# Order of the opening work in a per-batch adapter kernel: table rows, row picks and the second group of x

## The chip, the cores and the metric

The kernel runs on one core of one Trainium2 chip. The metric is the time of one execution on the device in microseconds (us); several runs are made and their median is given. A core has five engines that run their own instruction streams: TensorE (PE, matrix products), VectorE (DVE), ScalarE (ACT), GpSimd (POOL) and SyncE (SP, which here only issues DMAs). They wait for each other by semaphores.

## What is computed

There are 128 batches of a 128 x 512 tile of x. Each batch has a language id from 0 to 8 that chooses one of ten adapters: a product with W1 (512 to 128), ReLU, a product with W2 (128 to 512), a residual, a layer norm with the language's gamma and beta, and once more x. All in float32.

```python
w1 = W1[language_ids]
w2 = W2[language_ids]
h = jnp.einsum('bsh,bha->bsa', hidden_states, w1) + b1[language_ids][:, None, :]
h = jax.nn.relu(h)
adapted = jnp.einsum('bsa,bah->bsh', h, w2) + b2[language_ids][:, None, :]
x = hidden_states + adapted
mean = jnp.mean(x, axis=-1, keepdims=True)
var = jnp.mean(jnp.square(x - mean), axis=-1, keepdims=True)
normed = (x - mean) * jax.lax.rsqrt(var + LN_EPS)
return normed * gamma[language_ids][:, None, :] + beta[language_ids][:, None, :]
```

The result is x plus what this function returns for x.

## The kernel before

**Tiling.** A batch is one tile with its 128 rows on the 128 partitions. x is loaded in groups of four batches (`load_x`, 1 MB, four buffers), the output is stored in pairs. W1 and W2 of all ten languages (2.6 MB each) are loaded once and stay in SBUF.

**Tables.** beta, gamma and b2 have ten rows each, and a batch needs one row of each on all 128 partitions. So the kernel spreads all 30 rows over the partitions at the start, into `beta_b`, `gamma_b` and `b2_b`. The 30 rows are split into three bfloat16 parts that add up to the float32 value (`parts`, lines 133 to 137), and `pick` (lines 130 and 131) is a matrix of zeros and ones, made from the identity, that adds the three parts of one row. `spread(r, copier)` (line 151) is one matmul of TensorE into a PSUM tile `row`, of which there are five buffers (pool `p_y`, shared with the batches' results `py`), and one copy of it to the table, by VectorE (L160) or ScalarE (L158). Rows 0 to 9 are beta, 10 to 19 gamma, 20 to 29 b2.

**Order.** Each engine's order is written out by hand: `keep` chains an instruction behind the one before it on its engine. In the opening, TensorE runs 12 matmuls on a tile of ones without use for the result (`spin`), then the transposes of batch 0 (`transpose_x`) and of b1, then 22 rows. Every third row goes to ScalarE, the others to VectorE; after row 5 stand the transposes of batch 1, and after each later row a short `spin`. Then ScalarE stages W1 of batches 0 and 1 (`stage_w1`, L186: a copy of the language's W1 to a fixed buffer, three buffers), and for batches 0 to 3 there follow the four W1 products (`down`, L214, one PSUM buffer `ph`), the transposes of batch b + 2 for b below 2 (one PSUM buffer `pxT`), ReLU (`relu`, L222), the copy of the transposed x (`copy_xT`, L195) and the rows that are left, three per batch. Then come the W2 products of batches 0 and 1 (`up`, L231, with b2 added by a row matmul, L230, in the first four batches and in every fourth after).

**Main loop.** From `i = 3` each turn holds, in TensorE's order, transposes of batch i, W1 products of batch i - 1, W2 product of batch i - 2, while VectorE and ScalarE do the residual, the statistics and the scaling of earlier batches, and GpSimd adds b2 to x (`add_b2`, L201) and beta to x (`add_beta`, L208). The first transposes in the loop are those of batch 4, right behind the W2 product of batch 2; they are the first use of x's second group. GpSimd's first `add_b2` is that of batch 4 too.

**DMA.** SP issues in this order: language ids, gamma, batches 0 and 1 of x, W1 in four parts, batches 2 and 3 of x, W2 in two parts, then x's groups 1 to 3. ScalarE issues beta, b2 and b1. A load of several rows is shared by all 16 DMA engines, and whoever waits for it waits for all 16 shares.

**VectorE at the start.** Only ScalarE's and SP's first instructions and TensorE's are chained by `keep` in the opening; the VectorE lines 119 to 137 stand unchained and are issued as: memsets, language ids (L119 to L122, wait for the ids' DMA), parts (L133 to L137), then `both` and `pick` (L130, L131).

Of the kernel before, what the change touches and what calls it, by code (L numbers as in the profile page):

```python
# [8 lines left out]
FP = mybir.dt.float32  # L9
BF = mybir.dt.bfloat16  # L10
I32 = mybir.dt.int32
AF = mybir.ActivationFunctionType
ALU = mybir.AluOpType
# [3 lines left out]
P = 128  # L17
G = 4
# [5 lines left out]
def cond_resid_kernel(ctx: ExitStack, tc: tile.TileContext, x, itok, W1, b1, W2, b2, gamma, beta, out):  # L24
# [8 lines left out]
    nc = tc.nc  # L33
    B, S, H = x.shape
    L, _, A = W1.shape
# [7 lines left out]
    def keep(ins):  # L43

        engine = ins.ins.engine
        if engine in last:
            tc.add_manual_dep(ins.ins, last[engine], behind, reason="kept order")
        last[engine] = ins.ins.name
        return ins

    const = ctx.enter_context(tc.tile_pool(name="const", bufs=1))
    xp = ctx.enter_context(tc.tile_pool(name="xp", bufs=4))
# [4 lines left out]
    st = ctx.enter_context(tc.tile_pool(name="st", bufs=6))  # L57
# [5 lines left out]
    xs = {}  # L63

    def load_x(g):
        t = xp.tile([P, G, H], FP, tag="x", name=f"x_{g}")
        keep(nc.sync.dma_start(out=t, in_=x[g * G : (g + 1) * G].rearrange("b s h -> s b h")))
        xs[g] = t

    def xb(b):  # L70
        return xs[b // G][:, b % G, :]


    ids = const.tile([1, B], I32, name="ids")
    rows = rp.tile([P, H], FP, tag="r", name="rows")
# [3 lines left out]
    x_0 = xp.tile([P, G, H], FP, tag="x", name="x_0")  # L79
    xs[0] = x_0  # L80

    def load_part(lo, hi):
        keep(nc.sync.dma_start(out=x_0[:, lo:hi, :], in_=x[lo:hi].rearrange("b s h -> s b h")))

    keep(nc.sync.dma_start(out=ids, in_=itok.rearrange("(o b) -> o b", o=1)))
    keep(nc.scalar.dma_start(out=rows[0:L, :], in_=beta))
    keep(nc.sync.dma_start(out=rows[L : 2 * L, :], in_=gamma))
    keep(nc.scalar.dma_start(out=rows[2 * L : 3 * L, :], in_=b2))
    load_part(0, 2)
    keep(nc.scalar.dma_start(out=b1r, in_=b1))  # L90

    warm = const.tile([P, 1], FP, name="warm")
    nc.vector.memset(warm, 1.0)
    keep(nc.scalar.activation(warm, warm, AF.Sqrt))
    for k in range(KC):
        keep(
            nc.sync.dma_start(out=w1[:, :, k, :], in_=W1[:, k * P : (k + 1) * P, :].rearrange("l p a -> p l a"))
        )
    load_part(2, G)
    for l in range(0, L, 5):  # L100
        keep(
            nc.sync.dma_start(
                out=w2[:, l * H : (l + 5) * H].rearrange("p (l h) -> p l h", l=5),
                in_=W2[l : l + 5].rearrange("l a h -> a l h"),
            )
        )
    for g in range(1, 4):
        load_x(g)

    ident = const.tile([P, P], FP, name="ident")  # L110
# [4 lines left out]
    nc.gpsimd.memset(ones, 1.0)  # L115


    wrap = const.tile([1, B], I32, name="wrap")
    nc.vector.tensor_scalar(wrap, ids, 0, L, ALU.is_lt, ALU.mult)  # L119
    lang = const.tile([1, B], I32, name="lang")  # L120
    nc.vector.tensor_tensor(lang, ids, wrap, ALU.add)
    nc.vector.tensor_scalar(lang, lang, 0, L - 1, ALU.max, ALU.min)  # L122


    R = 3 * L
    parts = const.tile([P, H], BF, name="parts")
    nc.vector.memset(parts.bitcast(mybir.dt.uint32), 0)
    pick = const.tile([96, R], BF, name="pick")
    both = st.tile([P, R], FP, tag="both", name="both", bufs=1)[:96, :]
    nc.vector.tensor_tensor(both, ident[:96, 0:R], ident[:96, 32 : 32 + R], ALU.add)  # L130
    nc.vector.tensor_tensor(pick, both, ident[:96, 64 : 64 + R], ALU.add)  # L131
    left = rp.tile([P, H], FP, tag="r", name="left")
    nc.vector.tensor_copy(parts[0:R, :], rows[0:R, :])  # L133
    nc.vector.tensor_tensor(left[32 : 32 + R, :], rows[0:R, :], parts[0:R, :], ALU.subtract)
    nc.vector.tensor_copy(parts[32 : 32 + R, :], left[32 : 32 + R, :])
    nc.vector.tensor_tensor(left[64 : 64 + R, :], left[32 : 32 + R, :], parts[32 : 32 + R, :], ALU.subtract)
    nc.vector.tensor_copy(parts[64 : 64 + R, :], left[64 : 64 + R, :])  # L137

    b1T = const.tile([P, L], FP, name="b1T")

# [10 lines left out]
    def spread(r, copier):  # L151
        t = (beta_b, gamma_b, b2_b)[r // L]
        row = p_y.tile([P, H], FP, tag="y", name=f"row_{r}")
        pick_r = pick[:, r : r + 1].to_broadcast([96, P])
        keep(nc.tensor.matmul(row, lhsT=pick_r, rhs=parts[:96, :], start=True, stop=True))
        dst = t[:, r % L * H : (r % L + 1) * H]
        if copier is nc.scalar:
            keep(nc.scalar.copy(dst, row))  # L158
        else:
            keep(nc.vector.tensor_copy(dst, row))  # L160
# [22 lines left out]
    def stage_w1(b):  # L183
        w1s[b] = wp.tile([P, KC, A], FP, tag="w1s", name=f"w1s_{b}")
        src = w1.rearrange("p l k a -> p (l k a)")[:, bass.ds(lid(b, ET.Activation) * (KC * A), KC * A)]
        keep(nc.scalar.copy(w1s[b].rearrange("p k a -> p (k a)"), src))  # L186

    def transpose_x(b):
        pxs[b] = p_x.tile([P, KC, P], FP, tag="xT", name=f"pxT_{b}")
        for k in range(KC):  # L190
            keep(nc.tensor.transpose(pxs[b][:, k, :], xb(b)[:, k * P : (k + 1) * P], ident))  # L191

    def copy_xT(b):
        xT[b] = tp.tile([P, KC, P], FP, tag="xT", name=f"xT_{b}")
        keep(nc.scalar.copy(xT[b], pxs.pop(b)))  # L195
# [14 lines left out]
    def down(b):  # L210
        phs[b] = p_h.tile([P, P], FP, tag="h", name=f"ph_{b}")
        for k in range(KC):
            keep(
                nc.tensor.matmul(  # L214
                    phs[b], lhsT=w1s[b][:, k, :], rhs=xT[b][:, k, :], start=(k == 0), stop=(k == KC - 1)
                )
            )
        del xT[b], w1s[b]

    def relu(b):  # L220
        hT[b] = tp.tile([P, P], FP, tag="hT", name=f"hT_{b}", bufs=6)
        keep(nc.scalar.activation(hT[b], phs.pop(b), AF.Relu, bias=b1T[:, bass.ds(lid(b, ET.Activation), 1)]))  # L222
# [191 lines left out]
    def spin(n, width):  # L414
        idle = p_s.tile([P, H], FP, tag="s", name="idle")
        for _ in range(n):
            keep(
                nc.tensor.matmul(
                    idle[:, :width], lhsT=ones, rhs=ones[:, 0:1].to_broadcast([P, width]), start=True, stop=True
                )  # L420
            )


    spin(12, H)
    transpose_x(0)
    transpose_b1()
    copy_xT(0)
    for r in range(22):
        spread(r, nc.scalar if r % 3 == 2 else nc.vector)
        if r == 5:  # L430
            transpose_x(1)
            copy_xT(1)
        elif r > 5:
            spin(1, H // 2)
    stage_w1(0)
    stage_w1(1)
    spin(3, H)
    for b in range(4):
        down(b)
        if b < 2:  # L440
            transpose_x(b + 2)
        relu(b)
        if b < 2:
            copy_xT(b + 2)
        for r in range(22 + 3 * b, min(25 + 3 * b, R)):
            spread(r, nc.scalar if r % 3 == 2 else nc.vector)
        stage_w1(b + 2)
    up(0)
    up(1)
# [1 line left out]
    for i in range(3, B + U):  # L451
        if i < B and i % G == 0 and i // G + 3 < NG:
            load_x(i // G + 3)
        b = i - U - 1
# [19 lines left out]
        g, half = divmod(b, 2)  # L474
# [80 lines left out]
```

## Time and profile before

| | |
|---|---|
| median of 3 runs | 320.62 us (320.58 to 321.12) |
| the profiled execution | 321.39 us, span 318.8 us |
| TensorE matmul busy | 305.1 us (96%) |
| VectorE busy | 300.7 us (94%) |
| ScalarE busy | 285.5 us (90%) |
| GpSimd busy | 280.6 us (88%) |
| first 25 us: VectorE, ScalarE, GpSimd busy | 17.15, 13.87, 3.36 us |

The span runs from the first to the last instruction; the time of a run has what lies around it as well. A line of a timeline reads: start, duration, engine, source line, operation, output <- inputs with their sizes, how many in a row (x4), and in brackets how long the engine had stood idle before it and what it waited for. In the part on waits, "issue" is a wait for nothing that the profile shows. PEld is TensorE's weight load, which runs beside its matmuls. Part 2 of the page cuts the span in 40 slices and shows each engine's busy tenths.

### The profile page before, as it was taken

To read this page: it belongs to the slowest core of one execution; us is meant where nothing else is said; L and a number is where in the kernel's file an instruction comes from. 1 tells how busy PE (TensorE), PEld (TensorE's weight loads), DVE (VectorE), ACT (ScalarE), POOL (GpSimd) and SP (SyncE) were. 2 spreads that over 40 slices of the span, in tenths; PEclk is the share of its full clock that TensorE was granted. 3 is DMA by queue.
4 is the path that set the end of the run, shared out by engine and by line. 5 is a ranking of instruction groups with operands and counts; after the bars stand their busy time and mean duration, and the time that the engine had idled before them with its cause. 6 is when DMAs were issued, how large, how long until landed. Compare 5 with 4: busy or idle time off the path is not lost. (4 is left out here: it accounts for less than half of the span.)

```text
span 318.8 us, 7184 instructions
## 1 busy us (share of the span) xinstructions
PE 305.1 (96%) x1889; PEld 226.0 (71%) x1889; DVE 300.7 (94%) x1000; ACT 285.5 (90%) x721; POOL 280.6 (88%) x234
## 2 busy tenths in 40 slices
PE   8998999999999999999999999999999999999960
PEld 3475777777777777777777777777777777777730
DVE  5946999999999999999999999999999999999995
ACT  2686989999999999999999999999999999999972
POOL 1306999999999999999999999999999999999873
PEclk9999999999999999999999999999999999999995
DMA  7997577577766666678666676678766666633324
GB/s 204 317 386 288 198 262 254 214 264 263 221 231 212 223 246 232 228 264 263 247 215 213 217 244 231 223 265 264 245 210 215 224 241 228 226 135 133 129 112 156
DMA packets 40986, 72.88 MB, mean 229 GB/s; under 512 B 1737, under 2 KB 6868, under 8 KB 40946
## 3 DMA queue, kind: packets, MB, share of 16 engines
q1 hardware_dynamic: 40886, 72.38, 66.4%
q8 instruction: 15, 0.25, 0.3%
q14 instruction: 25, 0.20, 0.2%
q10 hardware_dynamic: 60, 0.05, 0.1%
HBM read 38.86 MB, written 33.55 MB: 227 GB/s over the span
## 5 line engine op out<-in xcount | busy, mean ns | idle before, releaser
L208 POOL TENSOR_TENSOR o<-x,beta_b 128x512 f32<-128x512 f32 x128 | 162.0, 1278 | 10.6 <-DVE beta_b L160 10.6
L201 POOL TENSOR_TENSOR r<-x,b_b 128x512 f32<-128x512 f32 x93 | 118.8, 1277 | 20.0 <-DMA x<-in_x_dram 12.1
L214 PE MATMUL ph<-xT,w1s 128*128 128x128 f32 x1024 | 135.7, 275 | 0.3 <-ACT w1s L186 0.2
L231 PE MATMUL py<-w,hT 128*128 x256 | 130.9, 593 | 0.2 <-DVE o L290 0.2
L214 PEld LDWEIGHTS ph<-xT,w1s 128*128 128x128 f32 x1024 | 124.6, 192 | 2.6 <-ACT hT L222 1.3
L191 PEld LDWEIGHTS pxT<-ident,x 128*128 128x128 f32 x512 | 63.9, 141 | 67.1 <-issue 43.4
L281 DVE SCALAR_TENSOR_TENSOR py<-py,nmean,gamma_b 128x512 f32<-128x512 f32 x126 | 94.7, 752 | 0.3 <-issue 0.3
L290 DVE SCALAR_TENSOR_TENSOR o<-py,rstd,o 128x512 f32<-128x512 f32 x122 | 90.4, 741 | 1.4 <-DVE nmean L242 0.5
L249 ACT ACTIVATE sq<-py,nmean 128x512 f32<-128x512 f32 x124 | 85.3, 688 | 4.5 <-DVE nmean L242 2.9
L195 ACT COPY xT<-pxT 128x512 f32<-128x512 f32 x128 | 73.8, 577 | 12.1 <-PE pxT L191 10.1
L186 ACT COPY w1s<-w 128x512 f32 x128 | 79.5, 622 | 0.2 <-DVE gamma_b L160 0.2
L191 PE MATMUL pxT<-ident,x 128*128 128x128 f32 x512 | 77.0, 273 | 0.9 <-ACT xT L195 0.7
L237 DVE SCALAR_TENSOR_TENSOR py<-py,r 128x512 f32<-128x512 f32 x93 | 64.7, 695 | 2.5 <-POOL r L201 0.6
L222 ACT ACTIVATE hT<-ph,b1T 128x128 f32<-128x128 f32 x128 | 47.6, 372 | 1.1 <-PE ph L214 1.0
L231 PEld LDWEIGHTS py<-w,hT 128*128 128x128 f32 x256 | 41.6, 192 | 2.9 <-issue 0.9
L237 DVE SCALAR_TENSOR_TENSOR py<-py,x 128x512 f32<-128x512 f32 x35 | 24.2, 692 | 3.7 <-PE py L231 3.7
L249 ACT ACTIVATION_READ_ACCUMULATOR sq<-py,nmean 128x1 f32 x124 | 25.2, 203 | 0.0
L255 ACT ACTIVATE sd<-ssq,eps 128x2 f32<-128x2 f32 x62 | 18.3, 296 | 2.1
L242 DVE TENSOR_SCALAR nmean<-sum 128x1 f32<-128x1 f32 x128 | 18.7, 146 | 0.2
L230 PE MATMUL py<-parts,pick 96*128 96x512 bf16 x35 | 13.3, 381 | 0.0
L237 DVE DVE_READ_ACCUMULATOR py<-py,r 128x1 f32 x93 | 13.1, 141 | 0.0
L270 DVE TENSOR_TENSOR stat<-stat,y 128x2 f32<-128x2 f32 x62 | 12.8, 206 | 0.0
(54 smaller groups left out, 117.7 us busy)
## 6 DMA issues: line engine op xcount, KB each, us to landing
x<-in_x_dram SPq DMA_DIRECT2D x31, 1024.0 KB, 6.1
out_dram<-o SPq DMA_DIRECT2D x61, 512.0 KB, 3.5
w<-in_L_cond_W_dram SPq DMA_DIRECT2D x4, 640.0 KB, 6.6
w<-in_L_cond_W_dram SPq DMA_DIRECT2D x2, 1280.0 KB, 11.5
out_dram<-o SPq DMA_DIRECT2D x6, 256.0 KB, 2.2
x<-in_x_dram SPq DMA_DIRECT2D x2, 512.0 KB, 3.9
rows<-in_L_cond_beta_dram ACTq DMA_DIRECT2D x1, 20.0 KB
rows<-in_L_cond_gamma_dram SPq DMA_DIRECT2D x1, 20.0 KB
```

The costliest lines, as they stand in the source:

```text
L186: keep(nc.scalar.copy(w1s[b].rearrange("p k a -> p (k a)"), src))
L191: keep(nc.tensor.transpose(pxs[b][:, k, :], xb(b)[:, k * P : (k + 1) * P], ident))
L195: keep(nc.scalar.copy(xT[b], pxs.pop(b)))
L201: keep(nc.gpsimd.tensor_tensor(rs[b], xb(b), b2_b[:, bass.ds(v * H, H)], ALU.add))
L208: keep(nc.gpsimd.tensor_tensor(os[g][:, j, :], xb(b), beta_b[:, bass.ds(v * H, H)], ALU.add))
L214: nc.tensor.matmul(phs[b], lhsT=w1s[b][:, k, :], rhs=xT[b][:, k, :], start=(k == 0), stop=(k == KC - 1))
L222: keep(nc.scalar.activation(hT[b], phs.pop(b), AF.Relu, bias=b1T[:, bass.ds(lid(b, ET.Activation), 1)]))
L231: keep(nc.tensor.matmul(ys[b], lhsT=hT[b], rhs=w2[:, bass.ds(v * H, H)], start=not m, stop=True))
L237: keep(nc.vector.scalar_tensor_tensor(ys[b], ys[b], 1.0, r, ALU.mult, ALU.add, accum_out=s))
L249: keep(nc.scalar.activation(sq, ys[b], AF.Square, bias=nmeans[b], accum_out=ssqs[g][:, j : j + 1]))
L281: nc.vector.scalar_tensor_tensor(ys[b], ys[b], nmeans.pop(b), gamma_b[:, bass.ds(v * H, H)], ALU.add, ALU.mult)
L290: nc.vector.scalar_tensor_tensor(o, ys.pop(b), rstds[g][:, j : j + 1], o, ALU.mult, ALU.add)
```

## The change

Five things are changed.

- `both` and `pick` are made before the language ids and the parts, and VectorE's opening instructions are chained by `keep` in that order.
- One long `spin` fewer at the start, and rows 0 and 1 go ahead of the transposes of batch 0.
- Rows alternate: even ones are copied by VectorE, odd ones by ScalarE, with one short `spin` per pair. The transposes of batch 1 stand after row 7.
- 24 rows are made before W1 is staged (22 before), and two per batch in batches 0 to 2 (three, three and two before).
- x's second group (batches 4 to 7) is loaded by two DMAs of two batches each, into the same tile.

```diff
--- before.py
+++ after.py
@@ -80,7 +80,8 @@
     xs[0] = x_0
 
     def load_part(lo, hi):
-        keep(nc.sync.dma_start(out=x_0[:, lo:hi, :], in_=x[lo:hi].rearrange("b s h -> s b h")))
+        dst = xs[lo // G][:, lo % G : lo % G + hi - lo, :]
+        keep(nc.sync.dma_start(out=dst, in_=x[lo:hi].rearrange("b s h -> s b h")))
 
     keep(nc.sync.dma_start(out=ids, in_=itok.rearrange("(o b) -> o b", o=1)))
     keep(nc.scalar.dma_start(out=rows[0:L, :], in_=beta))
@@ -90,7 +91,7 @@
     keep(nc.scalar.dma_start(out=b1r, in_=b1))
 
     warm = const.tile([P, 1], FP, name="warm")
-    nc.vector.memset(warm, 1.0)
+    keep(nc.vector.memset(warm, 1.0))
     keep(nc.scalar.activation(warm, warm, AF.Sqrt))
     for k in range(KC):
         keep(
@@ -104,7 +105,11 @@
                 in_=W2[l : l + 5].rearrange("l a h -> a l h"),
             )
         )
-    for g in range(1, 4):
+    x_1 = xp.tile([P, G, H], FP, tag="x", name="x_1")
+    xs[1] = x_1
+    load_part(G, G + 2)
+    load_part(G + 2, 2 * G)
+    for g in range(2, 4):
         load_x(g)
 
     ident = const.tile([P, P], FP, name="ident")
@@ -115,26 +120,27 @@
     nc.gpsimd.memset(ones, 1.0)
 
 
-    wrap = const.tile([1, B], I32, name="wrap")
-    nc.vector.tensor_scalar(wrap, ids, 0, L, ALU.is_lt, ALU.mult)
-    lang = const.tile([1, B], I32, name="lang")
-    nc.vector.tensor_tensor(lang, ids, wrap, ALU.add)
-    nc.vector.tensor_scalar(lang, lang, 0, L - 1, ALU.max, ALU.min)
-
-
     R = 3 * L
     parts = const.tile([P, H], BF, name="parts")
-    nc.vector.memset(parts.bitcast(mybir.dt.uint32), 0)
+    keep(nc.vector.memset(parts.bitcast(mybir.dt.uint32), 0))
     pick = const.tile([96, R], BF, name="pick")
     both = st.tile([P, R], FP, tag="both", name="both", bufs=1)[:96, :]
-    nc.vector.tensor_tensor(both, ident[:96, 0:R], ident[:96, 32 : 32 + R], ALU.add)
-    nc.vector.tensor_tensor(pick, both, ident[:96, 64 : 64 + R], ALU.add)
+    keep(nc.vector.tensor_tensor(both, ident[:96, 0:R], ident[:96, 32 : 32 + R], ALU.add))
+    keep(nc.vector.tensor_tensor(pick, both, ident[:96, 64 : 64 + R], ALU.add))
+
+
+    wrap = const.tile([1, B], I32, name="wrap")
+    keep(nc.vector.tensor_scalar(wrap, ids, 0, L, ALU.is_lt, ALU.mult))
+    lang = const.tile([1, B], I32, name="lang")
+    keep(nc.vector.tensor_tensor(lang, ids, wrap, ALU.add))
+    keep(nc.vector.tensor_scalar(lang, lang, 0, L - 1, ALU.max, ALU.min))
+
     left = rp.tile([P, H], FP, tag="r", name="left")
-    nc.vector.tensor_copy(parts[0:R, :], rows[0:R, :])
-    nc.vector.tensor_tensor(left[32 : 32 + R, :], rows[0:R, :], parts[0:R, :], ALU.subtract)
-    nc.vector.tensor_copy(parts[32 : 32 + R, :], left[32 : 32 + R, :])
-    nc.vector.tensor_tensor(left[64 : 64 + R, :], left[32 : 32 + R, :], parts[32 : 32 + R, :], ALU.subtract)
-    nc.vector.tensor_copy(parts[64 : 64 + R, :], left[64 : 64 + R, :])
+    keep(nc.vector.tensor_copy(parts[0:R, :], rows[0:R, :]))
+    keep(nc.vector.tensor_tensor(left[32 : 32 + R, :], rows[0:R, :], parts[0:R, :], ALU.subtract))
+    keep(nc.vector.tensor_copy(parts[32 : 32 + R, :], left[32 : 32 + R, :]))
+    keep(nc.vector.tensor_tensor(left[64 : 64 + R, :], left[32 : 32 + R, :], parts[32 : 32 + R, :], ALU.subtract))
+    keep(nc.vector.tensor_copy(parts[64 : 64 + R, :], left[64 : 64 + R, :]))
 
     b1T = const.tile([P, L], FP, name="b1T")
 
@@ -421,17 +427,21 @@
             )
 
 
-    spin(12, H)
+    def spread_turn(lo, hi):
+        for r in range(lo, hi):
+            spread(r, nc.scalar if r % 2 == 1 else nc.vector)
+            if r % 2 == 1:
+                spin(1, H // 2)
+
+    spin(11, H)
+    spread_turn(0, 2)
     transpose_x(0)
     transpose_b1()
     copy_xT(0)
-    for r in range(22):
-        spread(r, nc.scalar if r % 3 == 2 else nc.vector)
-        if r == 5:
-            transpose_x(1)
-            copy_xT(1)
-        elif r > 5:
-            spin(1, H // 2)
+    spread_turn(2, 8)
+    transpose_x(1)
+    copy_xT(1)
+    spread_turn(8, 24)
     stage_w1(0)
     stage_w1(1)
     spin(3, H)
@@ -442,8 +452,8 @@
         relu(b)
         if b < 2:
             copy_xT(b + 2)
-        for r in range(22 + 3 * b, min(25 + 3 * b, R)):
-            spread(r, nc.scalar if r % 3 == 2 else nc.vector)
+        for r in range(24 + 2 * b, min(26 + 2 * b, R)):
+            spread(r, nc.scalar if r % 2 == 1 else nc.vector)
         stage_w1(b + 2)
     up(0)
     up(1)
```

`load_part`, `spread`, `transpose_x`, `copy_xT`, `stage_w1` and `spin` are otherwise as they were. In the order that comes out, TensorE has five idle matmuls fewer (26 for 31), and SP has one DMA more.

## Prediction

> **What bounds the kernel now.** I read the page's part 2 first: from the fourth slice of 40 to the second-last TensorE is at 9 tenths, and VectorE and ScalarE nearly so. So the middle has a limit of its own, and what this change touches (the first 27 us) can only shift it. Next the timeline of TensorE late in the run, to get the pace and see whether anything waits there.
>
> ```profile
> 289.21 0.60 PE L191 MATMUL pxT<-ident,x 128*128 128x128 f32 x4
> ...
> 291.40 0.60 PE L191 MATMUL pxT<-ident,x 128*128 128x128 f32 x4
> ...
> 293.59 0.60 PE L191 MATMUL pxT<-ident,x 128*128 128x128 f32 x4
> ...
> 296.00 0.60 PE L191 MATMUL pxT<-ident,x 128*128 128x128 f32 x4
> ```
>
> Batches start every 2.19 us, every fourth 0.22 later (the extra row matmul): 8.98 us per four batches, with no wait. That is TensorE's own work: transposes 0.44, four W1 products 0.89, the W2 product 0.86. The end is therefore TensorE's first uninterrupted moment plus fixed work. The timeline of TensorE over the start finds that moment:
>
> ```profile
> 16.39 1.16 PE L214 MATMUL ph<-xT,w1s 128*128 128x128 f32 x8 [0.23 <-ACT w1s L186]
> ...
> 22.97 0.38 PE L230 MATMUL py<-parts,pick 96*128 96x512 bf16 x1
> 23.19 1.02 PE L231 MATMUL py<-w,hT 128*128 x2
> ...
> 25.34 1.02 PE L231 MATMUL py<-w,hT 128*128 x2
> 26.59 0.63 PE L191 MATMUL pxT<-ident,x 128*128 128x128 f32 x4 [0.22 <-DMA x<-in_x_dram]
> 27.89 0.66 PE L191 MATMUL pxT<-ident,x 128*128 128x128 f32 x4 [0.68 <-ACT xT L195]
> ```
>
> The first W1 product waits for the staged W1 (16.39). The transposes of batch 4 wait for x's second group (26.59), those of batch 5 for the only transpose buffer (27.89), and from there nothing waits. Why W1 is staged so late is in the timelines of VectorE and ScalarE:
>
> ```profile
> 5.40 0.42 DVE L137 CAST parts<-left 30x512 bf16<-30x512 f32 x1
> 5.85 0.19 DVE L130 TENSOR_TENSOR both<-ident 96x30 f32<-96x30 f32 x1
> 6.07 0.19 DVE L131 TENSOR_TENSOR pick<-both,ident 96x30 bf16<-96x30 f32 x1
> ...
> 7.57 4.28 DVE L160 COPY beta_b<-row 128x512 f32<-128x512 f32 x7 [0.15 <-PE row L155]
> 11.76 4.26 DVE L160 COPY gamma_b<-row 128x512 f32<-128x512 f32 x7
> ```
> ```profile
> 13.52 0.59 ACT L158 COPY gamma_b<-row 128x512 f32<-128x512 f32 x1 [0.79 <-PE row L155]
> 14.90 0.59 ACT L158 COPY b_b<-row 128x512 f32<-128x512 f32 x1 [0.79 <-PE row L155]
> 15.72 1.14 ACT L186 COPY w1s<-w 128x512 f32 x2 [0.24 <-DVE gamma_b L160]
> ```
>
> VectorE copies without a gap, 0.61 us a row, while ScalarE idles before each of its rows: VectorE's two rows in three set the pace.
>
> Last the DMA landings, from the semaphore increments in the trace (16 parts each): W1 complete at 14.43, x's batches 2 and 3 at 15.78, W2 at 22.56. Of x's second group fifteen parts landed by 25.23 and the last at 26.45. The DMA view of 20 to 32 us names the cause, one packet of TensorE's program (16 KB, 22.54 to 23.63) on one of the engines:
>
> ```profile
> q8 instruction: 1, 0.02, 0.6%
> ```
>
> **What the Trainium skill says.** *Runtime: NRT & Kernel Launch*, "Instruction fetch mechanics": a program is refilled in blocks of 256 instructions by a DMA queue of its own, mostly hidden. The trace has 16 such packets, about 18 us apart; that at 22.54 isn't hidden, it delays x by 1.22 us. *DMA: Bandwidth & Descriptors*, "Queues, rings and completion order": each DMA engine takes the queues in turn, packet by packet, so one late engine holds back the whole count of 16; that fits the lone late part. *VectorE: DVE Perf Modes*, its table of costs, gives 120 + 512 cycles for such a copy from PSUM, 0.66 us; the trace has 0.68 alone and 0.61 in a row. *TensorE: Matmul & The Clock Gate*, on the clock gate: 427 ns for 512 columns while cold. The trace agrees: twelve idle matmuls, 5.30 us.
>
> **The change part by part.**
>
> *Row picks ahead.* `both` and `pick` (0.19 each, about 0.44 of the chain) move into VectorE's wait for `ids` (1.18 us, until 2.35). They need `ident`, ready at 1.44, so they end near 1.9: no cost. The parts still end at 5.82, since `rows` holds their start at 3.07. One idle matmul less (11 x 0.427) ends at 5.88, so row 0 starts near 5.95 instead of 7.14. Rows 0 and 1 now go before the transposes of batch 0, whose result nobody needs before W1 is staged.
>
> *Rows in turn.* 24 rows are 12 copies for each engine. VectorE takes row 0 at about 6.5, the small b1T copy (0.17), row 2 at 7.45, then one per 0.61: row 22 starts at 7.45 + 10 x 0.61 = 13.5. ScalarE's row 23 can be made once VectorE has freed row 18's buffer (5 buffers; row 18 ends near 13.0) and is copied 13.5 to 14.1. TensorE has 2 x 0.22 + 0.11 = 0.55 per pair: hidden, just. With 0.24 for the language id and its waits ScalarE is ready at 14.35; W1 landed at 14.43, plus 0.1 for the semaphore: staging starts at 14.5, 1.2 earlier. W1's landing is now the limit there; a faster copy would bring no more.
>
> *Batches 0 to 3.* One row fewer for TensorE in batches 0 and 1 (0.22 each), but ScalarE's relu, xT, row and W1 stage take 1.98 per batch (relu at 17.59, 19.57, 21.55) and are as many as before. TensorE's 0.89 + 0.44 + 0.44 = 1.77 lies below that: no gain. So the whole stretch moves by 1.2, and TensorE is ready for W2 at about 21.75 instead of 22.95.
>
> *What is late next.* W2, at 22.56, which the change leaves where it is. Before, a landing took 0.15 to reach TensorE (26.45 to 26.59), and the W2 product starts 0.1 after its weight load: I take 22.8 against 23.19. Of the 1.2 us, 0.8 is lost in that wait and 0.39 stays. The bound below is 22.65, above is the rival on W2.
>
> *x's second group in halves.* Three W2 products take 2 x 1.08 + 0.86 = 3.02, so TensorE reaches batch 4 at 25.85. At 387 GB/s (the DMA view) half a group, 524 KB, is 1.35 us: the first half lands at 25.1 if the fetch delays it as it did the group, at 23.9 if not. Either is in time. The second half, at 26.45, is needed by batch 6's transposes (30.36 before). SP's added issue stands in a backlog of over 10 us (W2 issued at 11.07, landed 22.56) and costs nothing; if the backlog were gone, 0.4.
>
> So batch 4's transposes move from 26.59 to 25.85: 0.74. ScalarE's xT copy follows at once (the square of batch 0 before it moves by 0.39 and ends at 25.7), and batch 5's transposes with it. Rows alone would have left 26.59 standing, and halves alone give about 0.35 (TensorE was busy to 26.2). GpSimd's first sum with b2 starts 1.35 earlier, which buys room but no time, as GpSimd's 7 x 1.23 = 8.63 per four batches lies below TensorE's 8.98.
>
> *Sum.* 318.8 - 0.74 = 318.1 for the span, 320.65 for the profiled run (321.39). The median is 0.77 below that run; taking the same difference: 320.62 - 0.74 = **319.9 us**.
>
> **The rivals.**
>
> *A, W2 arrives late (slower).* Five idle matmuls less are ten instructions fewer, yet TensorE runs 1.2 us earlier there, so the same fetch may be asked for before W2's last part is through. Price: the 1.22 us seen on x, W2 at 23.8, its product at 24.05, batch 4 at 27.1: 0.5 late, 321.1. It decides once W2 lands after 23.3. For it: the fetch started within 0.3 us of W2's landing. Against: with a backlog on the engine the later fetches start near the end of the transfer in progress (45.04 inside the x landing 44.52 to 45.43), which points to 22.5 again.
>
> *B, half the gain.* The fetch catches only W2's tail, as at 45 us, where the last part came 0.45 after the others: W2 at 23.0, 0.3 gained: 320.3.
>
> *C, more.* TensorE lost 0.31 and 0.29 near batches 14 and 22, after two of VectorE's register loads took 1.20 (41.4) and 1.13 us (59.7) instead of 0.6. With GpSimd earlier and x's loads released sooner these may not recur: 319.3. Against: I see no cause for them, so they may as well recur.
>
> *D, rows not faster.* TensorE's 0.55 of 0.61 per pair leaves little; should ScalarE's rows come late by 0.05 each, W1 is staged 0.6 later, which the wait for W2 still swallows. It has no weight of its own.
>
> **How the numbers follow.** Forecast 0.47 (own range 319.5 to 320.3), C 0.21, B 0.17, A 0.15. About 0.2%, 0.64 us, is what can be told from no change, so faster means under 319.98: three quarters of the forecast and C, 0.57. Slower means over 321.26: A with a further slow register load, 0.3, and what I overlook, 0.13. The rest, 0.30, is same. The range goes from C with a little more, 319.1, to A, 321.1.
>
> **What would show it.** Right: W1 staged at 14.5; W2's first product at 22.8 with a wait for W2 before it; batch 4's transposes at 25.8 without a wait for x; 2.19 us per batch after. Wrong: a W2 landing beyond 23 (A or B), a wait for x before batch 4, row copies that don't alternate at 0.61, or a TensorE that waits again after batch 5.

## The result and the profile after

| | before | after |
|---|---|---|
| median of 7 runs each | 320.79 us (320.33 to 321.74) | 319.72 us (319.49 to 320.55) |
| the profiled execution | 321.39 us, span 318.8 us | 319.72 us, span 318.0 us |

The ratio is 0.9967, with an interval of [0.9952, 0.9982]: the kernel became 0.33% faster, between 0.18% and 0.48%. In microseconds the medians differ by 1.07.

The timelines of VectorE and of ScalarE after the change (start, duration, engine, line, operation, and in brackets the idle time before it) show that the opening does what was asked of it:

```profile
1.48 0.19 DVE L128 TENSOR_TENSOR both<-ident 96x30 f32<-96x30 f32 x1 [0.30 <-POOL ident masks.py:199]
1.70 0.18 DVE L129 TENSOR_TENSOR pick<-both,ident 96x30 bf16<-96x30 f32 x1
...
13.26 1.27 DVE L166 COPY b_b<-row 128x512 f32<-128x512 f32 x2
```
```profile
10.42 2.76 ACT L164 COPY gamma_b<-row 128x512 f32<-128x512 f32 x5
13.14 1.13 ACT L164 COPY b_b<-row 128x512 f32<-128x512 f32 x2
14.50 1.14 ACT L192 COPY w1s<-w 128x512 f32 x2 [0.23 <-DMA w<-in_L_cond_W_dram]
```

The picks end at 1.88, ScalarE copies its last seven rows without a gap where it had idled 0.24 to 0.79 us before most of its rows, and W1 is staged at 14.50, held by nothing but W1's own landing (14.38). TensorE's timeline shows what became of these 1.2 us:

```profile
15.17 1.16 PE L220 MATMUL ph<-xT,w1s 128*128 128x128 f32 x8 [0.55 <-ACT w1s L192]
...
22.64 1.10 PE L237 MATMUL py<-w,hT 128*128 x2 [0.73 <-DMA w<-in_L_cond_W_dram]
...
24.88 1.02 PE L237 MATMUL py<-w,hT 128*128 x2
25.74 0.60 PE L197 MATMUL pxT<-ident,x 128*128 128x128 f32 x4
27.01 0.66 PE L197 MATMUL pxT<-ident,x 128*128 128x128 f32 x4 [0.68 <-ACT xT L201]
...
285.78 0.60 PE L197 MATMUL pxT<-ident,x 128*128 128x128 f32 x4
...
294.76 0.60 PE L197 MATMUL pxT<-ident,x 128*128 128x128 f32 x4
```

There is a new wait of 0.73 us for W2 (landed 22.51) before the first W2 product, and none for x before the transposes of batch 4 at 25.74: the first half of x's second group landed by 25.19, the second half by 26.55. The pace is unchanged, 294.76 - 285.78 = 8.98 us for four batches.

The span fell by 0.89 us. (The times of the two profiled executions differ by 1.67, because 2.5 us lie around the span in that of before and 1.8 in that of after.) TensorE's and SP's timelines split the 0.89 in three. The transposes of batch 5, from which on TensorE has no wait of this kind, start 0.88 earlier (27.89 to 27.01). On the way to the last batch TensorE slips, that is, a batch starts later than the pace, by 0.23 us once instead of by 0.31 and 0.29: 0.37 more. And the end took back 0.35: from the last transposes to the end of the span it was 318.85 - 302.57 = 16.28 before and 317.96 - 301.33 = 16.63 after.

### The profile page after: what moved, and what is told of

Read it like the earlier page. It is cut to its first block, busy times and chain, and to the rows that moved or that the text cites. A ratio compares the mean times of both kernels' runs of the same rounds, so it can differ in the third digit from the quotient of the medians.

```text
span 318.0 us, 7173 instructions
## 1 busy us (share of the span) xinstructions
PE 302.7 (95%) x1883; PEld 225.0 (71%) x1884; DVE 297.9 (94%) x995; ACT 289.1 (91%) x726; POOL 280.6 (88%) x234
```

## The experiments

The theory at first was the prediction's own: the new order of the rows brings TensorE to W2 early, W2's landing takes two thirds of that, and the halves of x are needed to keep the rest. Each run below was timed next to runs of the kernel before on the same chip; since the median of the latter differs a little between the three sets (320.73, 320.70, 320.51), the ratios are what to compare. They are worked out from all runs and lie up to about 0.1% from the quotient of the two medians. Where two kernels were not timed in one set, overlapping intervals decide nothing.

| kernel | median us | ratio to before | W2 product, batch 4's and 5's transposes start |
|---|---|---|---|
| before, profiled again | 320.51 | 1.0003 [0.9992, 1.0015] | 22.57, 26.08, 27.39 |
| rows only | 320.72 | 1.0009 [0.9994, 1.0025] | 22.63, 26.17, 27.48 |
| halves only | 319.63 | 0.9967 [0.9959, 0.9976] | 22.75, 25.84, 27.11 |
| changed, picks late | 319.69 | 0.9966 [0.9955, 0.9977] | 22.41, 25.50, 26.77 |
| changed, fetch early | 320.65 | 1.0008 [0.9994, 1.0022] | 23.49, 26.59, 27.86 |
| before, no short idle matmuls | 319.70 | 0.9965 [0.9951, 0.998] | 22.56, 25.65, 26.92 |
| changed, five languages | 319.05 | 0.9949 [0.9936, 0.9962] | 21.89, 24.91, 26.18 |
| old rows, halves, five languages | 319.50 | 0.9961 [0.9947, 0.9975] | 22.40, 25.42, 26.69 |
| changed, W2 product later | 319.32 | 0.9960 [0.9947, 0.9972] | 22.45, 24.94, 26.49 |
| the same, no short idle matmuls | 318.96 | 0.9946 [0.9931, 0.9962] | 22.43, 24.44, 25.95 |
| the same, six more on VectorE | 318.39 | 0.9937 [0.9914, 0.9961] | 22.67, 24.68, 26.20 |
| old rows, halves, product later, no short idle | 318.21 | 0.9931 [0.9911, 0.9951] | 22.42, 24.43, 25.95 |

### The two halves of the change apart

Rows only: the changed kernel with x's second group loaded whole.

```diff
-    x_1 = xp.tile([P, G, H], FP, tag="x", name="x_1")
-    xs[1] = x_1
-    load_part(G, G + 2)
-    load_part(G + 2, 2 * G)
-    for g in range(2, 4):
+    for g in range(1, 4):
         load_x(g)
```

> The changed kernel with x's second group loaded whole again. Theory (the moment that counts is batch 4's transposes, and they need x): W1 is staged at 14.5 and W2's first product starts at 22.6 as in the changed kernel, but batch 4's transposes stay near 26.5, and the time is that of the kernel before within 0.3 us. Rival (the rows alone carry the gain): transposes near 25.8 and 0.8 us or more faster than before.

Halves only: the kernel before with that edit the other way round.

> The kernel before with x's second group in two halves and nothing else. Theory: TensorE itself is busy to 26.2, so batch 4's transposes start at 26.2 instead of 26.6 and the time falls by about 0.35 us; the two parts of the change together (0.85) bring more than the sum of each alone (0 and 0.35). Rival (halves are all that matters): 0.8 us faster.

Rows only gave nothing (1.0009). TensorE's timeline of that kernel:

```profile
22.63 1.10 PE L233 MATMUL py<-w,hT 128*128 x2 [0.73 <-DMA w<-in_L_cond_W_dram]
...
26.17 0.63 PE L193 MATMUL pxT<-ident,x 128*128 128x128 f32 x4 [0.29 <-DMA x<-in_x_dram]
```

It waits twice, for W2 and for x. (Batch 4 starts before the 26.5 expected, because x's second group was complete at 26.04 here.) Halves only gave all of the gain (0.9967, as the whole change). Here are TensorE's timelines, first of the kernel with halves only, then of the kernel before profiled again:

```profile
1.18 4.97 PE L423 MATMUL idle<-ones 128*128 128x512 bf16 x12 [1.18 <-POOL ones L120]
...
15.92 1.16 PE L219 MATMUL ph<-xT,w1s 128*128 128x128 f32 x8 [0.22 <-ACT w1s L191]
...
22.75 1.10 PE L236 MATMUL py<-w,hT 128*128 x2
...
25.84 0.60 PE L196 MATMUL pxT<-ident,x 128*128 128x128 f32 x4
```
```profile
1.18 4.57 PE L418 MATMUL idle<-ones 128*128 128x512 bf16 x12 [1.18 <-POOL ones L115]
...
15.61 1.16 PE L214 MATMUL ph<-xT,w1s 128*128 128x128 f32 x8 [0.22 <-ACT w1s L186]
...
22.57 1.10 PE L231 MATMUL py<-w,hT 128*128 x2
...
26.08 0.63 PE L191 MATMUL pxT<-ident,x 128*128 128x128 f32 x4 [0.26 <-DMA x<-in_x_dram]
```

> The kernel before, unchanged, for another profile of it. Theory (how late the old rows run depends on when TensorE's clock rises: the twelve idle matmuls took 5.30 us in the profile of before, but 4.97, 4.46 and 4.15 in three kernels that open alike): the first W1 product lies between 15.6 and 16.4 and the first W2 product 6.8 later, but not before W2 has landed, at 22.5 to 23.2; batch 4's transposes start at 26.3 to 26.6 in any case, because they wait for x; the time is 320.7. Rival (the opening of the kernel before is always as late as in its profile, and was earlier in the others through the halves or the idle matmuls left out): 16.4 and 23.2.

The first line carries part of the explanation. The same twelve idle matmuls took 5.30 us in the first profile of before, but 4.97 and 4.57 here, and 4.46, 4.34 and 4.15 in other kernels that open the same way: they come 0.43 us apart while TensorE's clock is low and 0.22 once it is up, and the moment at which it rises differs between executions. The old rows follow that moment: the first W1 product at 16.39, 15.92, 15.61, and the first W2 product at 23.19, 22.75, 22.57, that is, 6.8 to 7.0 later. The picks set a floor to this: where the idle matmuls took only 4.15 us (the old rows with five languages, below), TensorE waited 0.44 us for the picks, and the first W1 product started at 15.61 all the same. In the last two of the three profiles, TensorE comes to W2 just as it has landed (22.61 and 22.43), with no faster rows. The second profile of before also missed one expectation: batch 4 started at 26.08 and not at 26.3 to 26.6, because x's second group was complete at 25.95 instead of 26.45.

The new rows are done when W1 lands, and so TensorE reaches W2 too early to profit in full: 22.64 with a wait of 0.73, where the old rows give 22.57 with hardly one in the second profile of before and 23.19 in the first. At this point the new rows bring anything from nothing to 0.55 us, depending on the opening that they are compared with.

Which opening is the usual one isn't shown. The span of the first profile, 318.8, is that of most runs of before (medians of 318.9, 318.75 and 318.7 in the three sets); that of the second is 318.3, and none of its 14 runs has a shorter one. A rival to "W2's landing takes it all" is therefore that the new rows do gain at the start and lose as much at the end: from the last transposes to the end every profile with the new rows takes 0.34 to 0.59 us longer, except in one kernel that was changed for this (see the end of this part). The equal times of rows only and before, and of halves only and the whole change, speak for some of this, as a loss at the end without a gain at the start would show in them as about 0.1%; but that is less than their intervals can tell.

The picks, the smallest part of the change, can be undone without a loss that shows:

```diff
-    keep(nc.vector.tensor_tensor(both, ident[:96, 0:R], ident[:96, 32 : 32 + R], ALU.add))
-    keep(nc.vector.tensor_tensor(pick, both, ident[:96, 64 : 64 + R], ALU.add))
...
     keep(nc.vector.tensor_copy(parts[64 : 64 + R, :], left[64 : 64 + R, :]))
+    keep(nc.vector.tensor_tensor(both, ident[:96, 0:R], ident[:96, 32 : 32 + R], ALU.add))
+    keep(nc.vector.tensor_tensor(pick, both, ident[:96, 64 : 64 + R], ALU.add))
```

> The changed kernel with the two operations that make the row picks put back behind the rows' parts, all else as in the changed kernel. Theory: the first row and all behind it up to the staging of W1 come 0.4 to 0.45 us later (W1's first product at about 15.6 instead of 15.17), the wait for W2 in front of its first product (0.73) takes this in, and the time stays at 319.7. Rival (the picks' move is part of the gain): 320.1.

The first W1 product went from 15.17 to 15.61, as expected, and the first W2 product starts at 22.41 with hardly a wait, right behind the landing (22.27). The ratio, 0.9966, is about that of the changed kernel (0.9967).

### Is the wait for W2 what takes the rows' gain?

The two kernels of this pair leave languages 5 to 9 out: ids are clamped to 0 to 4 and half of W2 is loaded, so that W2 is there by 19.2. One has the new rows, the other the old, both have the halves.

```diff
-    for l in range(0, L, 5):
+    for l in range(0, L // 2, 5):
...
-    w2 = const.tile([P, L * H], FP, name="w2")
+    w2 = const.tile([P, L // 2 * H], FP, name="w2")
...
-    keep(nc.vector.tensor_scalar(lang, lang, 0, L - 1, ALU.max, ALU.min))
+    keep(nc.vector.tensor_scalar(lang, lang, 0, L // 2 - 1, ALU.max, ALU.min))
```

> The changed kernel with language ids limited to 0 to 4 and only the first half of W2 loaded; the other languages' batches are computed with language 4. Theory (W2's landing is what comes late next): W2 is there at 19.1, its first product starts when TensorE is ready, 21.75, batch 4's transposes at about 24.8, and the time falls by a further 0.85 us against the changed kernel. Rival (something else holds batch 4, such as the row copies or ScalarE): transposes stay near 25.7 and the time as in the changed kernel within 0.2 us.

> The kernel before with x's second group in halves and with half of W2 loaded (languages 5 to 9 are left out, ids are clamped to 0 to 4): the old order of rows, in the setting where W2 is no longer awaited. Theory (the new order of rows brings the first W1 product 0.75 to 1.2 us forward, and in the changed kernel W2's landing takes it all): the first W2 product starts at 22.75 to 23.0 and batch 4's transposes at 25.85 to 26.1, against 21.89 and 24.91 with the new rows in the same setting; the time is 319.6 to 319.9 against 319.05 there. Rival (the new order of rows is worth nothing in any setting): 319.05.

TensorE's timeline of the kernel with new rows, then of the one with old rows:

```profile
21.89 1.02 PE L237 MATMUL py<-w,hT 128*128 x2
...
24.91 0.60 PE L197 MATMUL pxT<-ident,x 128*128 128x128 f32 x4
```
```profile
22.40 1.02 PE L236 MATMUL py<-w,hT 128*128 x2
...
25.42 0.60 PE L196 MATMUL pxT<-ident,x 128*128 128x128 f32 x4
```

With W2 out of the way the new rows bring both starts forward by 0.51 us. So they are worth something at the start where nothing holds TensorE at W2; in the full kernel W2's landing takes this away where the old rows open as early as they do here. The size was below the 0.75 to 1.2 us expected: the old rows opened early here too (the idle matmuls took 4.15 us). Of the 0.51, the spans show only 0.1 (316.9 against 317.0, and TensorE slips in neither): the new rows lose the other 0.42 at the end, see below. The ratios, 0.9949 and 0.9961, overlap in their intervals.

### Why halves help: TensorE's program fetch

The prediction named one packet of TensorE's program, 16 KB, as the cause of x's late sixteenth share. Two runs move it. In the first, the kernel before loses the 16 short idle matmuls between its rows, 32 TensorE instructions with their weight loads, and keeps x's second group whole:

```diff
-        elif r > 5:
-            spin(1, H // 2)
```

> The kernel before, without the 16 single idle matmuls between its rows (32 TensorE instructions fewer), nothing else. Theory (TensorE's program fetch at 22.54 us is what made x's second group 1.2 us late, and halves help only because they get the first half past it): with fewer instructions the same fetch comes some microseconds later, the whole second group is complete at about 25.2 instead of 26.45, batch 4's transposes start without a wait for x at 25.85 to 26.3 (26.59 before), and the time falls by 0.3 to 0.8 us, to 320.0 to 320.4. Rival (a second group loaded whole is late for its size): x complete at about 26.1 or later and the time stays at 320.7.

TensorE's timeline of that kernel, and its page's DMA part for 20 to 25.5 us:

```profile
22.56 1.10 PE L231 MATMUL py<-w,hT 128*128 x2 [0.24 <-DMA w<-in_L_cond_W_dram]
...
25.65 0.60 PE L191 MATMUL pxT<-ident,x 128*128 128x128 f32 x4
```
```profile
DMA packets 1072, 2.13 MB, mean 387 GB/s; under 512 B 32, under 2 KB 32, under 8 KB 1072
...
q1 hardware_dynamic: 1072, 2.13, 104.9%
```

No program packet is left in this stretch (it comes at 28.9 instead), the whole group is complete at 25.13 instead of 26.45, and batch 4 doesn't wait. The last of the 16 shares comes 0.11 us after the fifteenth, where it came 1.22 and 0.86 after it in the two profiles of before. The second of those is the one to compare with, as its first W2 product starts at 22.57 too: there batch 4 starts at 26.08, here 0.43 earlier. The ratio of this kernel, 0.9965, is about that of the changed kernel, with neither the new rows nor the halves, and better than the 0.3 to 0.8 us expected, partly since TensorE came to W2 early here (22.56, right behind its landing). The Trainium skill, *Runtime: NRT & Kernel Launch*, "Instruction fetch mechanics", has the fetch of 256-instruction blocks mostly hidden behind execution. TensorE indeed never stops for it in the profile of before; what isn't hidden is its 1.1 us on one of 16 DMA engines, in front of a load that all 16 must finish.

In the second run the changed kernel gets 33 narrow idle matmuls more, of the same total width, so that the fetch comes earlier:

```diff
-    spin(11, H)
+    spin(44, P)
```

> The changed kernel with its 11 opening idle matmuls of 512 columns made 44 of 128 columns: the same TensorE time, 66 instructions more ahead of everything. Theory (a fetch of TensorE's program holds up whatever transfer stands behind it on its DMA engine): the 16 KB packet comes before W2's second part instead of after it, near 18.8 instead of 22.5; W2's last part lands near 23.7 instead of 22.5, batch 4's transposes start near 26.9 instead of 25.7, and the time is 1.1 us above the changed kernel's, at or above the kernel before. Rival (a fetch is hidden wherever it falls): W2 and the time as in the changed kernel within 0.2 us.

```profile
23.49 1.10 PE L237 MATMUL py<-w,hT 128*128 x2 [1.12 <-DMA w<-in_L_cond_W_dram]
...
26.59 0.60 PE L197 MATMUL pxT<-ident,x 128*128 128x128 f32 x4
```

TensorE's timeline shows the price. The fetch now stands at 17.1, in front of W2, whose last share lands at 23.36 (22.51 in the changed kernel); the W2 product and batch 4 are 0.85 late (1.1 was expected), and the whole gain is gone (1.0008, and the median too is about that of before). Five of its 22 runs took 322.4 to 323.2 us; the one profile, of a run of 320.36, doesn't show why. This was the prediction's rival A: its mechanism is real, its price 0.85 us, and it didn't happen in the changed kernel, where the fetch stayed at 22.5.

### A version that beats both

If the end is the moment from which TensorE runs without a wait plus fixed work, the 0.68 us for which batch 5's transposes wait behind batch 4's is next. Batch 2's W2 product can fill it:

```diff
-        if i == 4:
-            up(2)
         if i > 3 and on(i):
             transpose_x(i)
+        if i == 4:
+            up(2)
```

> The changed kernel with batch 2's W2 product issued after batch 4's transposes instead of before them. Theory (the end is TensorE's first uninterrupted moment plus fixed work, so the 0.68 us for which batch 5's transposes wait for batch 4's xT copy is still lost): batch 4's transposes start once the first half of x has landed, at about 25.3, the W2 product fills the wait, batch 5's transposes start at about 26.6 instead of 27.01, and the time falls by 0.4 us against the changed kernel, to about 319.3. Rival (W2's products set VectorE's work, and VectorE is as late as TensorE): no gain, 319.7.

> As the run before this one, and without the single idle matmuls between the rows (22 TensorE instructions fewer or more), so that the program fetch comes later. Theory: the first half of x is no longer delayed by the fetch and lands at about 24; batch 4's transposes start at 24.9, batch 5's at 26.25 instead of 27.01, and the time falls by 0.75 us against the changed kernel, to about 319.0. Rival (VectorE is as late as TensorE, or the fetch lands on another load that is waited for): 319.4 to 319.7.

The second run also leaves out the short idle matmuls between the rows. TensorE's timeline of each:

```profile
24.94 0.63 PE L197 MATMUL pxT<-ident,x 128*128 128x128 f32 x4 [0.31 <-DMA x<-in_x_dram]
...
25.63 1.02 PE L237 MATMUL py<-w,hT 128*128 x2
26.49 0.60 PE L197 MATMUL pxT<-ident,x 128*128 128x128 f32 x4
```
```profile
22.43 1.10 PE L237 MATMUL py<-w,hT 128*128 x2 [0.68 <-DMA w<-in_L_cond_W_dram]
...
24.44 0.60 PE L197 MATMUL pxT<-ident,x 128*128 128x128 f32 x4
...
25.09 1.02 PE L237 MATMUL py<-w,hT 128*128 x2
25.95 0.61 PE L197 MATMUL pxT<-ident,x 128*128 128x128 f32 x4
```

With the edit alone the W2 product fills the wait, and batch 4 waits for x again, whose first half the fetch delays (24.81). With the fetch moved to 27.7 that wait is gone too, and batch 5 starts at 25.95, 1.06 before the changed kernel. The times are those expected (319.32 and 318.96), though the intervals overlap with that of the changed kernel.

> The kernel before (old order of rows) with x's second group in halves, batch 2's W2 product after batch 4's transposes, and without the single idle matmuls between its rows. Theory (W2's landing takes all of what the new order of rows brings, and the new order costs 0.3 us in the last stores): W2's product at 22.45 to 22.7, batch 5's transposes at about 26.0 as with the new rows (25.95), a final wait 2.9 us after VectorE's last start, and a time of 318.65 to 318.9, no worse than the 318.96 of the same with the new rows. Rival (the new rows are worth something here): 319.3 to 319.5.

The same with the old rows, which is the kernel before with the halves, the moved product and without short idle matmuls, gave 318.21 us, 0.9931, less than the 318.65 to 318.9 expected. TensorE's timeline starts alike:

```profile
22.42 1.10 PE L236 MATMUL py<-w,hT 128*128 x2
...
24.43 0.60 PE L196 MATMUL pxT<-ident,x 128*128 128x128 f32 x4
...
25.09 1.02 PE L236 MATMUL py<-w,hT 128*128 x2
25.95 0.62 PE L196 MATMUL pxT<-ident,x 128*128 128x128 f32 x4
```

It has the lowest median of all and none of the new order. In the two profiles its span is 0.75 shorter than with the new rows: 0.27 by fewer slips of TensorE on the way, 0.48 from the last transposes to the end (16.15 against 16.63). In the same set of runs the changed kernel with late picks, which starts as the changed kernel does, had 319.69 and an interval that begins above where this one ends (0.9955 against 0.9951). Against the same kernel with new rows the intervals overlap.

### What the new rows cost at the end

From the start of VectorE's last operation to the moment at which SP has seen the last store land, every kernel with the new rows took 3.22 to 3.29 us, every one with the old rows 2.85 to 2.98. A suspect is an 8 KB program packet. With new rows it starts 0.6 us after VectorE's last operation has started, in the last stores, with old rows 1.3 us before; and by the traces' count it comes after some 1346 of VectorE's instructions, of which there are 1350 with the new rows and 1356 with the old. Six one-column memsets at VectorE's start make up for the difference:

```diff
-    keep(nc.vector.memset(warm, 1.0))
+    for _ in range(7):
+        keep(nc.vector.memset(warm, 1.0))
```

> The fastest kernel so far (the changed kernel, batch 2's W2 product after batch 4's transposes, no single idle matmuls; 318.96 us) with six more one-column memsets on VectorE at its very start, where it waits for the identity anyway; nothing else. In all kernels with the new order of rows the final wait comes 3.22 to 3.28 us after VectorE's last operation starts, in those with the old order 2.87 to 2.95. Theory (an 8 KB packet of VectorE's program, asked for near its 1346th instruction, falls into the last stores since the new order gives VectorE six instructions fewer): the packet moves back by some 1 us against the end, the final wait comes 2.9 us after, the time falls by 0.3 us to about 318.65. Rival (the last stores are slower for another reason, such as which engine's turn or the layout of the rows): 3.25 us and 318.96, or a little more by the six memsets.

The DMA view of the 2.25 us that follow the start of VectorE's last operation, without and with the six:

```profile
q1 hardware_dynamic: 335, 0.62, 73.0%
q14 instruction: 1, 0.01, 0.9%
```
```profile
q1 hardware_dynamic: 351, 0.65, 76.5%
```

The packet (q14) left the window as expected, which shows that it is VectorE's. The final wait fell from 3.23 to 3.05 us, half of what was expected, and the stretch from the last transposes to the end from 16.63 to 16.35 (16.15 to 16.28 in the six kernels with old rows, 16.62 to 16.74 in the seven with new ones). The ratio fell from 0.9946 to 0.9937, but the intervals overlap, and TensorE's slips, 0.39 us without the six and 0.06 with them, could make all of that difference. So one profile gives 0.2 to 0.3 us for the packet, the times can't confirm it, and what makes up the rest of the loss stays open.

## Why the prediction was right, and where it failed

**The time.** 319.9 was forecast and 319.72 measured, faster, inside the forecast's own range. The sum was made of one term, 0.74 us for batch 4's transposes. In the two profiles that term measured 0.85 (26.59 to 25.74), and two more that the sum didn't have nearly cancel, which is luck: 0.37 gained by slips, 0.35 lost at the end. The 0.77 us by which the profiled run of before lies above the median, and which the prediction took off, lie around the span and not in it: 2.5 us there, against 1.8 in most runs of before. (Two products and sums are off by a little: 22.8 + 3.02 is 25.82, and 7 x 1.23 is 8.61. Neither matters.)

**Row picks, rows in turn.** Held line by line: picks ended at 1.88 (1.9), staging began at 14.50 (14.5), W1's landing became its limit, batches 0 to 3 kept ScalarE's pace (1.97, then 1.76 between relus, for 1.98).

**What is late next.** Held: W2 landed at 22.51 and its product began at 22.64 after a wait, 0.16 earlier than the 22.8 taken.

**Halves.** Batch 4 at 25.74, for 25.85, without a wait for x. The fetch stood where it was expected and delayed the first half (to 25.19, for 25.1), which was in time.

**The step that failed** is the split: "Rows alone would have left 26.59 standing, and halves alone give about 0.35 (TensorE was busy to 26.2)". Rows alone gave nothing, as said, but halves alone gave 1.10 us (320.73 to 319.63), three times the 0.35 and as much as the whole change. Two terms were wrong. The 26.2, like the 0.39 us put down to the rows at W2, was read from one opening of before; with the same rows TensorE was through with its third W2 product at 25.66 in the second profile and at 25.84 with halves only. And the loss of the new rows at the end was put at nothing. How much of the 1.10 us is due to which isn't shown: the span with halves only is 0.58 shorter than in one profile of before and 1.13 shorter than in the other, of which batch 5's earlier start makes 0.28 and 0.78. The right reading of the change is: halves 0.33%, rows nothing on balance, with a loss at the end and a gain at the start of 0 to 0.55 us.

**The rivals.** A (W2 late through the fetch): real, but it needs the fetch well before W2's end. The run that put it at 17.1 lost 0.93 us; in the second profile of before it began at 21.79, and W2's last share landed at 22.43, only 0.09 after the one before it. B (half the gain by W2's tail): W2 landed at 22.51, no. C (fewer slips): half of it, 0.37 of the 0.60 in the pair of profiles. It isn't the change's doing as far as the runs show: slips of 0.06 to 0.6 us occur with old and new rows, and four profiles had none. D (rows late by 0.05 each): no.

## What to carry to other kernels

An opening that depends on the moment at which TensorE's clock rises can't be priced from one profile: compare the start of every stage in several profiles, and their spans with those of the other runs, before a gain is put down to a change of it. Before work is rearranged to start a stage sooner, ask what lands last in front of that stage; here W2's landing left at most 0.55 us of the 1.2 us that the faster rows had gained. Look at the end of the kernel too: a change of the opening cost some 0.4 us there. And where one share of 16 lands late, look for a program packet at that moment: leaving out 32 instructions that do nothing moved it, and that was worth as much as the change.

## What the hardware showed beyond that

- The rise of TensorE's clock came between 2.8 us (kernel with five languages and old rows) and 5.4 us (before) after the first of twelve idle matmuls, in programs that open alike. The Trainium skill, *TensorE: Matmul & The Clock Gate*, "Part 1", says that the window that decides it runs free of the kernel's start and gives a scatter of 0.5 us to either side; these runs fit the first and show a wider scatter.
- TensorE's slips in the main loop come after slow register loads on VectorE, most of them 9 to 10 us after. Of 32 such loads the median took 0.61 us. In four of the fourteen profiles none took over 0.8 us between 35 and 65 us, and there TensorE slipped by nothing; in the ten others the slowest one there took 0.98 to 1.52 us, and TensorE slipped by 0.06 to 0.60 us. In the changed kernel no slip followed a load of 1.05 us at 49.3, though. Neither what makes a load slow nor whether it causes the slip was tried.
